# Layer 2 attention on one core: softmax halves merged on 32 partitions, three score buffers, all context keys made ahead

## The chip, the cores and the metric

The kernel runs on one core of a Trainium2 chip. The metric is the device time of one execution in microseconds (us); the time shown for a kernel is the median of its runs. A core has TensorE (PE in the profile, its weight loads PEld), VectorE (DVE), ScalarE (ACT), GpSimd (POOL) and SyncE (SP, which only issues DMAs here). Each works through its own instruction stream in order, and they wait for each other through semaphores. SBUF has 128 partitions; TensorE writes into PSUM[...].

## The reference

Four layers, each an attention and a feed-forward part with residuals, on x of 4x256x256 (batch, tokens, width) with a context of 4x1601x256. Only the attention of layer 2 is touched by the change:

```python
def _L2_xattn_ref(x, h_ctx_kv, wq, wk, wv, wo, wk_ctx, wv_ctx, q_norm_w, k_norm_w):
    # 16 query heads, 4 key heads, head width 128
    q = (x @ wq).reshape(B, L, NUM_HEADS, HEAD_DIM)
    k = (x @ wk).reshape(B, L, NUM_KV_HEADS, HEAD_DIM)
    v = (x @ wv).reshape(B, L, NUM_KV_HEADS, HEAD_DIM)
    q = rms_norm(q, q_norm_w)
    k = rms_norm(k, k_norm_w)
    k_ctx = (h_ctx_kv @ wk_ctx).reshape(B, T, NUM_KV_HEADS, HEAD_DIM)
    v_ctx = (h_ctx_kv @ wv_ctx).reshape(B, T, NUM_KV_HEADS, HEAD_DIM)
    k_ctx = rms_norm(k_ctx, k_norm_w)
    q = q * cos + rotate_half(q) * sin
    k = k * cos + rotate_half(k) * sin
    k_full = jnp.concatenate([k_ctx, k], axis=1)
    v_full = jnp.concatenate([v_ctx, v], axis=1)
    ...
    mask = jnp.concatenate([jnp.zeros((L, T), x.dtype), causal], axis=1)
    scores = jnp.einsum('blhd,bmhd->bhlm', q, k_full) * scale + mask
    probs = jax.nn.softmax(scores, axis=-1)
    out = jnp.einsum('bhlm,bmhd->blhd', probs, v_full)
    return out.reshape(B, L, NUM_HEADS * HEAD_DIM) @ wo
...
x = x + _L2_xattn_ref(_layernorm(x, axis=-1), ctx_2048, ...)
```

## The kernel before

Layer 2 attention is worked off in sixteen units, one for each batch entry and key head (`units`), with four query heads in each unit. The keys of a unit are 1601 of the context and 256 of its own, cut into 15 tiles of 128 (`NK2`); tiles 0 to 11 and 96 rows of tile 12 are context.

*Context keys made ahead.* `l2_early` is a generator that makes the context keys and values of the first 15 units (`EARLY`) in small pieces: products, norm, transposes, and stores to DRAM. Earlier layers call `fill` to run pieces of it beside their own work. What is left over runs while the first unit is prepared, and `for _ in self.early: pass` ends it before the first score.

*Preparation of a unit.* `prep` is a generator too: query products and their rope (two pieces, `tpq`), products of the own keys (`tpkv`, tiles 12 and 13, then 14), the square root for the norms, and transposes of the queries (`tpqT`) and the keys (`tpk`). A unit that was made ahead loads its context part from DRAM; the sixteenth makes it in `prep` itself, with six more `tpkv` and three more `tpk` pieces. While a unit's heads run, the pieces for the next unit are drawn by tables: `WHEN_EARLY` says how many in each of the eight steps (two steps for each head).

*A head.* Its 256 queries are worked in four chunks of 64 (`scores`, c from 0 to 3). The keys of a chunk are spread over partitions: four column groups of 32 in the array write four partition groups of a score tile (two PSUM banks), so each query's scores lie on four partitions, j, 32+j, 64+j and 96+j. VectorE adds the causal mask to the last tiles (L1489) and takes the maximum of each partition (L1492). ScalarE takes the exponential with that maximum and sums it (L1496). Maxima go to `nm`, sums to `sm`, both 128x8, a column for each group of 32 queries.

*The merge.* The four partial maxima and sums of a query have to be joined (`merge`). TensorE transposes `nm` and `sm` into PSUM (L1507, L1508). VectorE takes the smallest of the negated maxima (L1512) and differences (L1514); ScalarE exponentiates them (L1515); VectorE weights the sums, adds them, takes the reciprocal and multiplies (L1517 to L1521). TensorE transposes the result back (L1523) and VectorE copies it to `rm` (L1525). Then GpSimd scales the probabilities by `rm` (L1532, eight instructions a head), VectorE transposes them in blocks of 32x32 into `pT` (L1538), TensorE multiplies by the values (tile `o`), and after four heads `project` multiplies by `wo` and L1559 adds to the residual.

*Order.* The loop at the end of `l2_xattn` runs these beside each other: in each step the scores of one head, a step of the softmax of the head before it (`softmax_steps`), value products of the head before that (`value_steps`), and pieces of `prep`. The tile framework's scheduler then orders the instructions of each engine by its own estimate, except those that are pinned (`keep_in_program_order`). PSUM: two score tiles (four banks), two banks for `prep` and `project` (tag `tp`), one for the merge, one for `o`.

Of the kernel before, what the change touches and what calls it, by code (L numbers as in the profile page):

```python
# [23 lines left out]
P = 128  # L24
# [28 lines left out]
EARLY = 15  # L53
# [5 lines left out]
class Kernel:  # L59
# [1210 lines left out]
    def l2_xattn(self):  # L1270
# [11 lines left out]
        with ExitStack() as es:  # L1282
            one = es.enter_context(tc.tile_pool(name="a2one", bufs=1, reuse_waits="tile"))
            two = es.enter_context(tc.tile_pool(name="a2", bufs=2, reuse_waits="tile"))
            ps_s = es.enter_context(tc.tile_pool(name="a2s", bufs=2, space=PSUM))
            ps = es.enter_context(tc.tile_pool(name="a2p", bufs=2, space=PSUM))
            ps_m = es.enter_context(tc.tile_pool(name="a2m", bufs=1, space=PSUM))
# [6 lines left out]
            kw = one.tile([P, 1], F32, name="kw")  # L1294
            nc.scalar.dma_start(kw, i["l2_knw"].rearrange("o p -> p o"))
# [17 lines left out]
            def turned(b):  # L1313

                xn = self.xn.tile([P, 2, D], F32, name="xn")
                self.layernorm(xn, self.x[b])
                if b == 0:
                    self.fill(LN2)
                tp = ps.tile([P, 2, 2, P], F32, name="tp_ln", tag="tp")
                for k in range(2):  # L1320
                    for q in range(2):
                        nc.tensor.transpose(tp[:, k, q, :], xn[:, q, k * P : (k + 1) * P], self.ident)
                t = self.xnT.tile([P, 2, S], F32, name="xT2", tag="xnT")
                nc.scalar.copy(t, tp.rearrange("p k q t -> p k (q t)"))
                return t

            def swapped(ap):
# [5 lines left out]
            def load(g, early):  # L1333
                w = {}
                for n, shape in (("wq", [P, 2, 512]), ("wkc", [P, 2, 256]), ("wks", [P, 2, 256])):
                    if n == "wkc" and early:
                        continue
# [9 lines left out]
            def prep(u, w, ctxT, res):  # L1347
# [3 lines left out]
                early = u < EARLY  # L1351
                va = two.tile([P, NK, HD2], F32, name="va2", bufs=3)
                kT = two.tile([P, NK, P], F32, name="kT2")
                if early:
                    kd, vd = self.early_kv[u]
                    for t, d in ((kT, kd), (va, vd)):
                        nc.sync.dma_start(t[:, :CT, :], d[:, :CT, :])
                    nc.sync.dma_start(kT[:, CT, :96], kd[:, CT, :96])
                    nc.sync.dma_start(va[:96, CT, :], vd[:96, CT, :])
# [4 lines left out]
                kr = one.tile([P, NK, HD2], F32, name="kr2")  # L1364
                ss = self.small.tile([P, NK + 8], F32, name="ss2")
                ra, rb = tabs["l2_qnw"]
                qo = []
                for q in range(2):
# [6 lines left out]
                    nc.vector.tensor_reduce(ss[:, NK + 4 * q : NK + 4 * q + 4], sq, AX.X, ALU.add)  # L1375
# [11 lines left out]
                def squares(m0, m1):  # L1387
                    n = m1 - m0
                    sq = one.tile([P, 4, HD2], F32, name="sq2")
                    nc.scalar.activation(sq[:, :n, :], kr[:, m0:m1, :], AF.Square)  # L1390
                    nc.vector.tensor_reduce(ss[:, m0:m1], sq[:, :n, :], AX.X, ALU.add)

                if early:
                    nc.gpsimd.memset(kr[:96, CT, :], 0.0)
                for ms in ((12, 13), (14,), (0, 1), (2, 3), (4, 5), (6, 7), (8, 9), (10, 11)):
                    if early and ms[0] < CT:
                        continue
                    tp = ps.tile([P, 2, 256], F32, name="tpkv", tag="tp")
                    rows = P
                    for n, m in enumerate(ms):  # L1400
                        for k in range(2):
                            if m < CT:
                                self.mm(tp[:, n, :], ctxT[:, k, m * P : (m + 1) * P], w["wkc"][:, k, :], k == 0, k == 1)
                            elif m == CT and early:
                                pass
                            elif m == CT:
                                self.mm(tp[:96, n, :], ctxT[:, k, m * P : m * P + 96], w["wkc"][:, k, :], k == 0, k == 1)
# [3 lines left out]
                        if m == CT:  # L1411
                            for k in range(2):
                                self.mm(tp[96:, n, :], xb[:, k, :32], w["wks"][:, k, :], k == 0, k == 1)
                    m, n = ms[0], len(ms)
                    if m == CT and early:
                        for t, v in ((kr, tp[:, :, :HD2]), (va, tp[:, :, HD2:])):
                            nc.scalar.copy(t[96:, CT, :], v[96:, 0, :])
                            nc.scalar.copy(t[:, CT + 1, :], v[:, 1, :])
                    else:
                        nc.scalar.copy(kr[:rows, m : m + n, :], tp[:rows, :n, :HD2])  # L1420
                        nc.scalar.copy(va[:rows, m : m + n, :], tp[:rows, :n, HD2:])
                    if rows < P:
                        nc.gpsimd.memset(kr[rows:, m, :], 0.0)
                    if m == CT + 2:
                        ra, rb = tabs["l2_knw"]
                        ko = one.tile([P, 3, HD2], F32, name="ko2")
                        t2 = one.tile([P, 3, HD2], F32, name="kt2")
                        own = kr[:, CT:, :]
                        nc.gpsimd.tensor_tensor(ko, own, ra, ALU.mult)
                        nc.vector.tensor_tensor(halves(t2), swapped(own), halves(rb), ALU.mult)  # L1430
                        nc.gpsimd.tensor_tensor(ko, ko, t2, ALU.add)
                    if m in (2, 6, 10, 14):
                        squares(CT if m == 14 else m - 2, m + n)
                    yield
                m0 = CT if early else 0
                self.rstd(ss[:, m0:], ss[:, m0:], 1.0 / HD2, self.eps6)
                rq = two.tile([P, 8], F32, name="rq2")
                nc.vector.tensor_scalar(rq, ss[:, NK:], 1.0 / math.sqrt(HD2), None, ALU.mult)
# [4 lines left out]
                for m in range(0, 0 if early else CT, 4):  # L1443
                    nc.gpsimd.tensor_tensor(
                        kr[:, m : m + 4, :], kr[:, m : m + 4, :], ss[:, m : m + 4, None].to_broadcast([P, 4, HD2]), ALU.mult
                    )
                for m in range(3):
                    nc.scalar.activation(ko[:, m, :], ko[:, m, :], AF.Copy, scale=ss[:, CT + m : CT + m + 1])
# [8 lines left out]
                for m0 in (12,) if early else (0, 4, 8, 12):  # L1457
                    tp = ps.tile([P, 4, P], F32, name="tpk", tag="tp")
                    n = min(4, NK - m0)
                    for m in range(n):  # L1460
                        nc.tensor.transpose(tp[:, m, :], kr[:, m0 + m, :] if m0 < CT else ko[:, m, :], self.ident)
                    if m0 < CT:
                        nc.scalar.activation(kT[:, m0 : m0 + 4, :], tp, AF.Copy, scale=kw)
                    elif early:
                        nc.scalar.copy(kT[:, CT, 96:], tp[:, 0, 96:])
                        nc.scalar.copy(kT[:, CT + 1 :, :], tp[:, 1:n, :])
                    else:
# [772 lines left out]
```

## Time and profile before

| what | us |
|---|---|
| median of 3 runs | 2660.19 (2654.16 to 2660.89) |
| the profiled execution, time | 2609.97 |
| the profiled execution, span from first to last instruction | 2608.2 |
| layer 2 attention in it: first score 670.3, last residual add starts 1778.67 | about 1109 |
| the last context-key work of `l2_early` in it | to about 671 |

Times inside the kernel come from one profiled execution; its mean granted TensorE clock is 0.979. A residual add (L1559) closes each unit, so that the sixteen of them, at 780.0, 847.9, 917.3, 985.2, 1053.7, 1121.6, 1190.9, 1258.9, 1327.3, 1395.3, 1464.6, 1532.5, 1601.0, 1677.1, 1740.7 and 1778.7 us, mark the pace of the stage. Matmuls are pipelined in the records, so that a TensorE that shows as busy is not always streaming. A float32 matmul shows as two records.

### The profile page before, as it was taken

To read this page: it belongs to the slowest core of one execution; us is meant where nothing else is said; L and a number is where in the kernel's file an instruction comes from. 1 tells how busy PE (TensorE), PEld (TensorE's weight loads), DVE (VectorE), ACT (ScalarE), POOL (GpSimd) and SP (SyncE) were. 2 spreads that over 40 slices of the span, in tenths; PEclk is the share of its full clock that TensorE was granted. 3 is DMA by queue.
4 is the path that set the end of the run, shared out by engine and by line. 5 is a ranking of instruction groups with operands and counts; after the bars stand their busy time and mean duration, and the time that the engine had idled before them with its cause. 6 is when DMAs were issued, how large, how long until landed. Compare 5 with 4: busy or idle time off the path is not lost. (4 is left out here: it accounts for less than half of the span.)

```text
span 2608.2 us, 47024 instructions
## 1 busy us (share of the span) xinstructions
PE 2472.6 (95%) x17800; PEld 1512.2 (58%) x17816; DVE 1473.9 (57%) x3039; ACT 1307.1 (50%) x2955; POOL 751.9 (29%) x1030
## 2 busy tenths in 40 slices
PE   7989978999899999999999999998998999999997
PEld 4678967777455555555555555655564544545553
DVE  6344537635677777777777777673334314334323
ACT  2335545424544445444544454532326766857775
POOL 1015646132444334334334444332102001011000
PEclk8999999899999999999999999998999999999998
DMA  5155686626311111111111110004211100000000
GB/s 203 61 190 164 187 174 206 202 67 211 114 47 39 47 47 47 47 42 36 46 46 39 47 47 21 9 1 165 99 60 55 34 1 28 4 4 2 6 6 5
DMA packets 94654, 186.24 MB, mean 71 GB/s; under 512 B 15052, under 2 KB 62864, under 8 KB 93232
## 3 DMA queue, kind: packets, MB, share of 16 engines
q1 hardware_dynamic: 78278, 144.90, 16.4%
q0 software_dynamic: 10416, 28.46, 4.9%
q10 hardware_dynamic: 5738, 9.87, 1.2%
q8 instruction: 145, 2.38, 0.4%
q14 instruction: 77, 0.63, 0.1%
HBM read 136.77 MB, written 46.42 MB: 70 GB/s over the span
## 5 line engine op out<-in xcount | busy, mean ns | idle before, releaser
L1496 ACT ACTIVATE p<-s,nm 128x448 f32<-128x448 f32 (+1 forms) x512 | 326.9, 645 | 423.4 <-DVE nm L1492 259.1
L1957 ACT ACTIVATE e<-s 128x1024 f32<-128x1024 f32 (+1 forms) x448 | 404.3, 960 | 158.2 <-PE s L76 153.1
L76 PE MATMUL s<-kT,qT 128*32 128x448 f32 (+1 forms) x4096 | 470.2, 556 | 10.0 <-ACT p L1496 5.0
L76 PE MATMUL o<-pT,va 128*128 128x256 f32 (+2 forms) x1920 | 431.0, 376 | 6.1 <-DVE pT L1538 6.1
L1532 POOL TENSOR_SCALAR p<-p,rm 128x448 f32<-128x448 f32 (+1 forms) x512 | 323.3, 659 | 369.5 <-DVE rm L1525 339.2
L76 PEld LDWEIGHTS o<-pT,va 128*128 128x128 f32 (+1 forms) x1920 | 344.4, 191 | 93.0 <-issue 51.5
L1538 DVE STREAM_TRANSPOSE pT<-p 128x896 f32<-128x896 f32 (+1 forms) x256 | 283.8, 1127 | 37.2 <-POOL p L1532 33.5
L1492 DVE TENSOR_REDUCE nm<-s 128x2 f32<-128x896 f32 (+1 forms) x256 | 282.6, 1104 | 3.3
L76 PE MATMUL s<-qb,kT 32*128 32x256 f32 (+1 forms) x3328 | 267.6, 404 | 13.2 <-ACT e L1957 11.0
L76 PEld LDWEIGHTS s<-kT,qT 128*32 128x32 f32 x4096 | 123.6, 109 | 265.0 <-issue 223.4
L76 PE MATMUL o<-e,va 128*32 128x256 f32 (+1 forms) x3328 | 235.7, 391 | 1.2 <-DVE os L2054 1.2
L76 PEld LDWEIGHTS s<-qb,kT 32*128 32x128 f32 (+1 forms) x3328 | 162.9, 181 | 105.0 <-issue 75.4
L76 PEld LDWEIGHTS o<-e,va 128*32 128x32 f32 (+1 forms) x3328 | 90.5, 110 | 115.0 <-issue 74.9
L1984 POOL TENSOR_TENSOR x<-x,t 128x32 f32<-128x32 f32 x64 | 14.7, 252 | 438.4 <-DVE t L1979 438.4
L76 PE MATMUL fill<-wkc_early,ctxT 128*128 128x256 f32 (+1 forms) x532 | 130.7, 394 | 8.2 <-ACT kT_early L1252 7.8
L1489 DVE TENSOR_TENSOR s<-s,mask 128x128 f32<-128x128 f32 (+1 forms) x256 | 83.0, 325 | 67.5 <-PE s L76 62.8
L76 PEld LDWEIGHTS fill<-wkc_early,ctxT 128*128 128x128 f32 (+1 forms) x532 | 102.0, 196 | 26.2 <-ACT kT_early L1252 10.3
L431 POOL DMA_INDIRECT f0xr<-f0xd,f0src x95 | 92.0, 968 | 50.8 <-PE f0tph L488 42.3
L1384 POOL TENSOR_TENSOR qo<-qo,qt 128x512 f32<-128x512 f32 x32 | 41.1, 1284 | 225.2 <-DVE rm L1525 139.7
L1496 ACT ACTIVATION_READ_ACCUMULATOR p<-s,nm 128x1 f32 x512 | 101.7, 199 | 0.0
L76 PE MATMUL f2gu<-f2wgu,f2xsT 128*128 x176 | 85.6, 611 | 0.6 <-issue 0.3
L529 POOL DMA_INDIRECT f0yt<-f0yd,f0slot x64 | 66.8, 1044 | 47.5 <-DMA vd<-va_early 16.3
(517 smaller groups left out, 3567.4 us busy)
## 6 DMA issues: line engine op xcount, KB each, us to landing
ctxT<-in_ctxT SPq DMA_DIRECT2D x10, 1664.0 KB, 10.6
f0yd<-f0ys SPq DMA_DIRECT2D x95, 128.0 KB, 2.8
vd<-va_early SPq DMA_DIRECT2D x90, 128.0 KB, 2.5
kd<-kT_early SPq DMA_DIRECT2D x45, 256.0 KB, 2.5
kT<-kd SPq DMA_DIRECT2D x15, 768.0 KB, 4.2
va<-vd SPq DMA_DIRECT2D x15, 768.0 KB, 6.0
wq<-in_l_wq SPq DMA_DIRECT2D x16, 512.0 KB, 3.3
wo<-in_l_wo SPq DMA_DIRECT2D x16, 512.0 KB, 3.1
```

Source lines behind the costliest of these rows:

```text
L76: self.nc.tensor.matmul(out, lhsT, rhs, start=start, stop=stop, **kw)
L431: nc.gpsimd.indirect_dma_start(out=t, out_offset=None, in_=xd[:, :], in_offset=bass.IndirectOffsetOnAxis(ap=src[:, n : n + 1], axis=0),)
L529: nc.gpsimd.indirect_dma_start(out=yt, out_offset=None, in_=yd[:, :], in_offset=bass.IndirectOffsetOnAxis(ap=slot[:, t, r : r + 1], axis=0),)
L1384: nc.gpsimd.tensor_tensor(o1, o1, t2, ALU.add)
L1489: nc.vector.tensor_tensor(sv, sv, mask[:, 2 * c : 2 * c + 2, : nt - CT, :].rearrange("p n t i -> p n (t i)"), ALU.add)
L1492: nc.vector.tensor_reduce(nm[:, 2 * c : 2 * c + 2], s[:, :, : nt * 32], AX.X, ALU.max, negate=True)
L1496: nc.scalar.activation(p[:, n, : nt * 32], s[:, n, : nt * 32], AF.Exp, bias=nm[:, e : e + 1], accum_out=sm[:, e : e + 1],)
L1532: nc.gpsimd.tensor_scalar(p[:, n, : nt * 32], p[:, n, : nt * 32], r[:, e : e + 1], 1.0, ALU.mult, ALU.mult)
L1538: nc.vector.transpose(pT[:, 2 * c : 2 * c + 2, :nt, :].rearrange("p n t i -> p n (t i)"), p[:, :, : nt * 32])
L1957: nc.scalar.activation(e[:kr, :, :n, :], s[t][:kr, :, :n, :], AF.Exp, scale=1.0 / math.sqrt(HD3))
L1984: nc.gpsimd.tensor_tensor(xt, xt, t[:, q], ALU.add)
```

## The change

The merge no longer goes over TensorE. Maxima and sums of a head lie in one tile (`nmsm2`, 128x2x8). Four GpSimd copies bring its four partition groups side by side onto 32 partitions, VectorE and ScalarE join them there, and four GpSimd products write the shares `rm2` back to the four partition groups. The bank that the merge held, and one of the two of tag `tp`, make a third score tile. All sixteen units are made ahead, so that `prep` has no path of its own for context keys. The tables draw mostly one piece of `prep` per step. After each square root a tiny pinned exponential makes ScalarE load the exponential table at once.

```diff
-EARLY = 15
+EARLY = B * NKV2
...
-            ps_s = es.enter_context(tc.tile_pool(name="a2s", bufs=2, space=PSUM))
-            ps = es.enter_context(tc.tile_pool(name="a2p", bufs=2, space=PSUM))
-            ps_m = es.enter_context(tc.tile_pool(name="a2m", bufs=1, space=PSUM))
+            ps_s = es.enter_context(tc.tile_pool(name="a2s", bufs=3, space=PSUM))
+            ps = es.enter_context(tc.tile_pool(name="a2p", bufs=1, space=PSUM))
...
                 self.layernorm(xn, self.x[b])
+                exps_next()
...
+            def exps_next():
+
+                self.pin(nc.scalar.activation(self.small.tile([P, 1], F32, name="one2"), self.eps6, AF.Exp))
...
-                for ms in ((12, 13), (14,), (0, 1), (2, 3), (4, 5), (6, 7), (8, 9), (10, 11)):
-                    if early and ms[0] < CT:
-                        continue
+                for ms in ((12, 13), (14,)):
...
-                m0 = CT if early else 0
-                self.rstd(ss[:, m0:], ss[:, m0:], 1.0 / HD2, self.eps6)
+                self.rstd(ss, ss, 1.0 / HD2, self.eps6)
+                exps_next()
...
-            def merge(nm, sm):
-
-
-                t = ps_m.tile([P, 512], F32, name="tm2")
-                ct, st = t[:8, 0:P], t[:8, P : 2 * P]
-                tc.keep_in_program_order(nc.tensor.transpose(ct, nm, self.ident))
-                tc.keep_in_program_order(nc.tensor.transpose(st, sm, self.ident))
-                by = lambda ap: ap.rearrange("n (a j) -> n j a", a=4)
-                wide = lambda ap: ap[:, :, None].to_broadcast([8, 32, 4])
-                lo = self.small.tile([8, 32], F32, name="lo2")
-                nc.vector.tensor_reduce(lo, by(ct), AX.X, ALU.min)
-                e = self.small.tile([8, P], F32, name="em2", bufs=2)
-                nc.vector.tensor_tensor(by(e), wide(lo), by(ct), ALU.subtract)
+            def merge(ms):
+
+
+
+                c = self.small.tile([32, 4, 2, 8], F32, name="ms2")
+                for a in range(4):
+                    nc.gpsimd.tensor_copy(c[:, a], ms[32 * a : 32 * a + 32])
+                by = lambda ap: ap.rearrange("j a n -> j n a")
+                wide = lambda ap: ap[:, None, :].to_broadcast([32, 4, 8])
+                lo = self.small.tile([32, 8], F32, name="lo2")
+                nc.vector.tensor_reduce(lo, by(c[:, :, 0]), AX.X, ALU.min)
+                e = self.small.tile([32, 4, 8], F32, name="em2")
+                nc.vector.tensor_tensor(e, wide(lo), c[:, :, 0], ALU.subtract)
                 nc.scalar.activation(e, e, AF.Exp)
-                w = self.small.tile([8, P], F32, name="wm2", bufs=2)
-                nc.vector.tensor_tensor(w, e, st, ALU.mult)
-                tot = self.small.tile([8, 32], F32, name="tot2")
+                yield
+                w = self.small.tile([32, 4, 8], F32, name="wm2")
+                nc.vector.tensor_tensor(w, e, c[:, :, 1], ALU.mult)
+                tot = self.small.tile([32, 8], F32, name="tot2")
                 nc.vector.tensor_reduce(tot, by(w), AX.X, ALU.add)
                 nc.vector.reciprocal(tot, tot)
-                nc.vector.tensor_tensor(by(e), by(e), wide(tot), ALU.mult)
-                yield
-                nc.tensor.transpose(t[:, 256:264], e, self.ident[:8, :8])
                 r = self.small.tile([P, 8], F32, name="rm2")
-                nc.vector.tensor_copy(r, t[:, 256:264])
+                for a in range(4):
+                    nc.gpsimd.tensor_tensor(r[32 * a : 32 * a + 32], e[:, a], tot, ALU.mult)
                 return r
...
-            WHEN = [2, 2, 2, 3, 2, 0, 2, 2]
-            WHEN_EARLY = [0, 1, 1, 2, 1, 0, 2, 1]
-            BETWEEN = [0, 0, 0, 0, 0, 0, 1, 1]
+            WHEN = [0, 1, 1, 1, 2, 0, 1, 1]
+            BETWEEN = [0, 0, 0, 0, 0, 0, 0, 1]
...
-                        if pieces is not None and not early:
+                        if pieces is not None:
                             for _ in range(BETWEEN[step]):
                                 next(pieces, None)
```

## The prediction

> **What bounds the kernel now.** I read the page first, then a table of stretches, the waits, and the order of time inside one head. The page (busy time and share of each engine) and the table of stretches (length, then busy us of TensorE, weight loads, VectorE, ScalarE, GpSimd; clock, DMA share, GB/s), cut at the residual adds of L1559, which mark one unit each:
>
> ```profile
> PE 2472.6 (95%) x17800; PEld 1512.2 (58%) x17816; DVE 1473.9 (57%) x3039; ACT 1307.1 (50%) x2955; POOL 751.9 (29%) x1030
> ...
> 780.00:1601.00 821.00, 814.99 (x5240) 451.71 (x5236) 628.83 (x1063) 391.81 (x1104) 329.73 (x479) 1.00 0.13 44
> 1601.00:1677.10 76.10, 76.00 (x483) 46.84 (x479) 54.39 (x92) 36.24 (x102) 29.25 (x41) 1.00 0.02 7
> 1677.10:1740.70 63.60, 61.89 (x431) 35.57 (x427) 46.95 (x79) 28.01 (x81) 21.14 (x33) 1.00 0.03 9
> ```
>
> The first stretch is twelve units: 68.4 us each, TensorE covered 99% of the time, VectorE 52.4 us a unit. TensorE sets the pace, and the 76.1 us unit is the one in which the context keys of the last unit are made.
>
> The waits of VectorE in the middle of the stage, and one head in order of time (start, us, engine, line, operation, count, idle before and releaser):
>
> ```profile
> DVE wm L1517 <- ACT em L1515: 80.9, 50, 2.5
> ...
> 1126.57 0.29 ACT L1515 ACTIVATE em<-em 8x128 f32<-8x128 f32 x1
> 1126.89 0.28 DVE L1517 TENSOR_TENSOR wm<-em,tm 8x128 f32<-8x128 f32 x1 [1.40 <-ACT em L1515]
> 1127.20 0.38 DVE L1519 TENSOR_REDUCE tot<-wm 8x32 f32<-8x128 f32 x1
> 1127.90 0.99 PE L76 MATMUL s<-kT,qT 128*32 128x480 f32 x2
> 1128.82 0.22 PE L1523 MATMUL tm<-ident,em 8*128 8x8 f32 x1
> 1128.98 3.42 PE L76 MATMUL s<-kT,qT 128*32 128x480 f32 x30
> 1129.42 5.05 POOL L1532 TENSOR_SCALAR p<-p,rm 128x448 f32<-128x448 f32 x8 [8.96 <-DVE rm L1525]
> 1130.85 0.37 DVE L1489 TENSOR_TENSOR s<-s,mask 128x192 f32<-128x192 f32 x1 [1.59 <-PE s L76]
> 1131.12 1.10 DVE L1538 STREAM_TRANSPOSE pT<-p 128x896 f32<-128x896 f32 x1
> 1132.15 1.12 DVE L1492 TENSOR_REDUCE nm<-s 128x2 f32<-128x960 f32 x1
> 1134.47 1.12 DVE L1492 TENSOR_REDUCE nm<-s 128x2 f32<-128x960 f32 x1
> 1135.51 2.21 DVE L1538 STREAM_TRANSPOSE pT<-p 128x960 f32<-128x960 f32 x2
> 1137.12 0.21 ACT L1496 ACTIVATION_READ_ACCUMULATOR p<-s,nm 128x1 f32 x1
> ```
>
> Two things are to be seen. The merge's last transpose (tm) falls inside a run of score matmuls; the two chunks take from 1127.90 to 1132.33, 4.4 us, where an unbroken pair takes 3.43 (at 1109.99). And VectorE stands 1.4 us for the small exponential, which hurts nobody now.
>
> **What the Trainium skill says.** "TensorEngine Tiling (Array Packing)", Key Properties: changing the tiling mode drains TensorE; the trace agrees, a step between the 32-column scores and full-width work costs about 0.1 us beyond streaming. "GPSIMD Engine Reference", 3.1: two-input elementwise work costs about 2.6 cycles per element there, plus a dispatch per instruction. "ScalarE: Activation LUTs", What ACT_TABLE_LOAD costs: about 1283 ns a load, as here (1.28); its further 1.38 us drain is not visible here (load 1104.43, square root 1105.73).
>
> **The change, part by part.** I call T a transpose, k a mask add, M a maximum.
>
> *Off TensorE.* Per head two transposes (1123.52 to 1123.74, 0.22 us) and the third. In the built order of before, three heads of four have the third inside a quad of scores (cost 4.43-3.43 = 1.0 us), one has it between values (0.3). Per unit: 4x0.22+3x1.0+0.3 = 4.2 us. TensorE alone would then need about 64 us a unit.
>
> *VectorE's new order.* In the built program the five merge operations of a head (lo, em, wm, tot, reciprocal) stand in one piece, directly behind the head's last maximum and ahead of the T of that head and of the next masks. Before, they were spread over the next head's masks and maxima. So VectorE, in order, now waits out the whole chain: last exponentials, four GpSimd copies, em's exponential, then four GpSimd products and the first two scalings before the first T. That is a loop in which nothing of one head overlaps the next on VectorE. Its wait L, from the end of the last M to the first T:
> - exponentials of the last chunk: 0.11 to start plus 1.41 (1135.92 to 1137.33) = 1.52; semaphore 0.10
> - four copies of 32x16 on GpSimd. No row has them. GpSimd's 128x32 product takes 252 ns, two of them 0.46 us; 24 elements fewer at the skill's 2.6 cycles and 1.2 GHz is 0.05 less, so 0.16 start to start, 0.20 for the last: 0.7 (bounds 0.45 and 1.05)
> - VectorE's small work: the router's softmax (128x32 at 1794.67 to 1795.84) has the same operations: 0.22, 0.23, exponential 0.26, 0.23, 0.22, 0.20, plus 0.08 in: 1.44
> - 0.16 to GpSimd, four 32x8 products 0.67 (bounds 0.45 and 1.05), two scalings 1.26, hops 0.06: 2.15
>
> L = 1.52+0.10+0.70+1.44+2.15 = 5.9 us.
>
> Start to start a T is 1.03 (1131.12 to 1132.15) or 1.1 in the pair, a free k 0.27, k with its M behind it 0.37, M 1.04. A head's four T, four k, four M: 2.06+2.21+0.54+0.74+3.12+1.12 = 9.8 us. The four heads of a unit in the new order:
> - head 0: 9.8
> - head 1: plus two rounds of query work behind the first T, 6x0.6 (sum, two products): 13.4
> - head 2: one k and one M move in front of the first T, under L (-1.3); rope and squares of the own keys +1.1, reciprocal +0.2: 9.8
> - head 3: 9.8, its residual add hidden under L
>
> Sum 42.8. ScalarE delays two of the waits: in head 2 both table loads, the filler exponential (0.2) and three scalings of ko come ahead of the exponentials of chunks 2 and 3, +1.5; in head 3 a query copy stands ahead of the last, +0.5. Behind the copies and products on GpSimd nothing else is queued but this head's scalings; the two query scalings (1.04 each) that stand ahead of the copies in head 2 end within the +1.5. Layernorm once in four units: 0.7. Unit: 42.8+2.0+0.7+4x5.9 = 69.1, taken as 69.0, against 68.4. VectorE is late next, with TensorE some 4 us a unit idle. Where TensorE idles most: tpk's copy to kT now stands behind the merge's exponential, with only two value matmuls to cover it.
>
> *Third score buffer, single bank for prep pieces.* Nothing: no large wait on a score buffer before, and each prep piece has half a head to be emptied. TensorE's pieces find the bank free in the hand-made order by 0.3 us or more, except one (second query transpose, 1.4 us), inside TensorE's slack. Bounds -10 and +10 us.
>
> *Exponential table reloaded at once.* The same loads, earlier: the copies of ko stand between it and the maxima anyway. Counted in the +1.5.
>
> *Sixteenth unit early.* 52 matmul records (28 took 6.31 us, so 0.22 each) and 13 transposes at 0.11: 12.9 us ahead of the first score. The stretch 645 to 670 holds about 7 us in which TensorE waits for the prep of unit 0; I let 5 be filled: +8 (bounds +4 and +14; the last unit's norm and turns can stand alone). In return the 76.1 us unit becomes an ordinary one. SP's queue loses one context load and one weight load and gains this unit's stores and reads; the DMA share there is 2 to 13%, so I cost that at nothing.
>
> *Sum*, on the profiled execution (span 2608.2, time 2609.97). Before: first score 670.3 to the last residual add's end 1779.4, 1109.1. After: first head to its last M 8 (scores 1.7, four k and M 5.6, hops), fifteen units 15x69.0 = 1035.0, three heads without prep (14.4, 14.4, 15.7: one k and M hidden in the first two) 44.5, tail L 5.9 + T paced by the scalings 4.9 + values, projection, add as at 1767.55 to 1779.4, 11.8 = 22.6. Together 1110.1, +1; with the start +8: **+9**. The median shown, 2660.19, is 50 us above the profiled execution, for a reason that the profile doesn't give; I add the +9 to it: **2669**.
>
> **Rivals.** (1) *Faster: L is shorter than added up and TensorE's relief is passed on.* For it: small GpSimd memsets follow at 34 ns, and 4.2 us a unit are really gone from TensorE, the bound; were VectorE no bound, 15x4.2 would be saved. Against it: five engine hops remain. 63 heads turn on L, so 0.1 us is 6 us; it decides below L = 5.6. At L = 5.5: 9-25 = -16, 2644. If the timed runs are longer because TensorE's clock is lower in them, before is hurt more than VectorE's loop, which helps this case. (2) *GpSimd's small operations are dear*: 0.26 start to start, like its two memsets in a row (1106.31, 1106.57). Eight times 0.09 makes L 6.6: +41, in all +50, 2710. For it: partition moves, never seen here; against: the 128x32 product. (3) *The start doesn't hide*: +14 instead of +8, 2675; it shifts any case and is in the range.
>
> **How the numbers follow.** Forecast (L 5.6 to 6.3, difference -8 to +34; own range 2652 to 2694) 0.45, of it 0.17 within 8 us and 0.28 slower; rival 1 0.28; rival 2 0.27. What a measurement of this kernel can tell from no change is 0.3%, 8 us. So faster 0.28, same 0.17, slower 0.55. The range reaches from a little below rival 1 to rival 2: 2636 to 2712.
>
> **What would show it.** Right: VectorE waits of 2 us and more, once a head, for GpSimd's copies (before lo) and scalings (before the first T); units of 69 us with TensorE's coverage down by some 4 us each; no unit of 76 us; first score at about 678. Wrong: TensorE still without gaps and units of 67 us or less (rival 1); GpSimd copies 0.25 us apart (rival 2); VectorE's waits for TensorE's scores at the top.

## The result and the profile after

The changed kernel takes 2666.78 us in the median of 22 runs (2654.13 to 2671.25), the kernel before beside it 2658.49 us (22 runs). The ratio is **1.0032, 95% interval 1.0022 to 1.0041**: 8.3 us slower (5.8 to 10.9). That is about the 0.3%, 8 us, that the prediction took as the least that can be told from no change. A later group of runs (e11 below) gave 1.0033 (1.0022 to 1.0044), so the loss is small but real.

The profiled execution of the changed kernel has a span of 2666.0 us, that of the kernel before one of 2608.2. These 58 us aren't the effect of the change. The two programs are the same up to layer 2, and most of the difference is there: the first query product of layer 2 starts at 652.0 us before and at 695.7 us after. Two further profiles, of later groups (e8, the kernel before, 657.8; e11, the changed kernel, 658.7), show no such difference. The level ahead of layer 2 goes with the group of runs: each of the groups e1 to e4, e5 to e8 and e9 to e12 ran on one chip of its own, and this start is at 686 to 691 us in the first group and at 651 to 659 in the other two. Whether it is the chip or the hour that does it was not tried. So spans of different groups aren't compared below, only ratios to the kernel before on the same chip, and stretches of the trace that begin in layer 2.

The first line of the page of the changed kernel (busy time, share of the span and instructions of each engine):

```profile
PE 2448.7 (92%) x17609; PEld 1503.6 (56%) x17625; DVE 1397.0 (52%) x2912; ACT 1304.6 (49%) x2986; POOL 844.7 (32%) x1545
```

The table of stretches of the changed kernel, cut at the residual adds as for the kernel before (length, then busy us of TensorE, weight loads, VectorE, ScalarE, GpSimd; clock, DMA share, GB/s). The first line holds twelve units, the second and third one unit each:

```profile
839.70:1668.00 828.30, 773.40 (x5092) 435.43 (x5088) 574.01 (x966) 389.10 (x1119) 399.23 (x864) 1.00 0.14 44
1668.00:1734.70 66.70, 62.44 (x407) 35.64 (x407) 46.63 (x75) 31.32 (x91) 32.34 (x67) 1.00 0.04 14
1734.70:1803.40 68.70, 64.96 (x459) 36.70 (x451) 45.57 (x76) 25.36 (x78) 31.30 (x78) 1.00 0.03 8
```

A unit takes 828.30/12 = 69.03 us, where it took 68.42 before. TensorE is covered 93% of the stretch instead of 99%: it lost (814.99-773.40)/12 = 3.5 us of covered time per unit, and the unit still became longer. VectorE has less to do as well, 47.8 us per unit instead of 52.4. No engine is full any more, so something waits. The unit of 76.1 us is gone: the two stretches after the twelve take 66.7 and 68.7 us. VectorE's waits in the same twelve units of the changed kernel (total, times, longest):

```profile
DVE lo L1478 <- POOL ms L1474: 136.2, 48, 3.5
DVE pT L1503 <- POOL p L1497: 94.2, 48, 2.5
DVE wm L1484 <- ACT em L1481: 14.2, 48, 0.3
```

Each happens once a head, 48 times: 2.8 us until GpSimd's copies are done (which themselves wait for the head's last exponentials), 2.0 us for the scaled pieces, 0.3 us for the small exponential. Together they are 20.4 us per unit. With its 47.8 us of work VectorE is taken up for 68.2 of the 69.03 us: these waits are the pace. Before, the largest of its waits was 1.6 us per head for em's exponential (80.9 us in 50), which hurt nobody because TensorE was late.

One merge of the changed kernel in order of time (start, us, engine, line, operation, count, idle before and what ended it):

```profile
1194.72 1.16 DVE L1458 TENSOR_REDUCE nmsm<-s 128x2 f32<-128x960 f32 x1
...
1196.91 0.67 ACT L1462 ACTIVATE p<-s,nmsm 128x480 f32<-128x480 f32 x1
...
1197.74 0.88 POOL L1474 COPY ms<-nmsm 32x16 f32<-32x16 f32 x4 [7.67 <-ACT p L1462]
...
1198.65 0.20 DVE L1478 TENSOR_REDUCE lo<-ms 32x8 f32<-32x32 f32 x1 [2.77 <-POOL ms L1474]
...
1199.10 0.23 ACT L1481 ACTIVATE em<-em 32x32 f32<-32x32 f32 x1 [1.10 <-DVE em L1480]
...
1199.36 0.18 DVE L1484 TENSOR_TENSOR wm<-em,ms 32x32 f32<-32x32 f32 x1 [0.29 <-ACT em L1481]
...
1199.80 0.19 DVE L1487 RECIPROCAL tot<-tot 32x8 f32<-32x8 f32 x1
...
1200.14 0.96 POOL L1490 TENSOR_TENSOR rm<-em,tot 32x8 f32<-32x8 f32 x4 [1.52 <-DVE tot L1487]
...
1201.19 5.06 POOL L1497 TENSOR_SCALAR p<-p,rm 128x448 f32<-128x448 f32 x8
...
1202.49 1.11 DVE L1503 STREAM_TRANSPOSE pT<-p 128x896 f32<-128x896 f32 x1 [2.50 <-POOL p L1497]
...
1203.52 0.27 DVE L1455 TENSOR_TENSOR s<-s,mask 128x128 f32<-128x128 f32 x1
```

The last maximum ends at 1195.88 and the first transpose starts at 1202.49. In these 6.61 us VectorE works for 0.9 us. The next head's first scores, which TensorE began at 1199.71 (3.2 us for two chunks), lie ready from about 1201.3 (an estimate: half of the 3.2 us), but their mask stands behind that transpose in VectorE's order and runs at 1203.52.

### The profile page after: what moved, and what is told of

Same layout as the page of the kernel before. It is cut to its first block, busy times and chain, and to the rows that moved or that the text cites. A ratio compares the mean times of both kernels' runs of the same rounds, so it can differ in the third digit from the quotient of the medians.

```text
span 2666.0 us, 46991 instructions
## 1 busy us (share of the span) xinstructions
PE 2448.7 (92%) x17609; PEld 1503.6 (56%) x17625; DVE 1397.0 (52%) x2912; ACT 1304.6 (49%) x2986; POOL 844.7 (32%) x1545
## 5 line engine op out<-in xcount | busy, mean ns | idle before, releaser
L1462 ACT ACTIVATE p<-s,nmsm 128x448 f32<-128x448 f32 (+1 forms) x512 | 326.2, 644 | 511.6 <-DVE nmsm L1458 464.6
L76 PE MATMUL s<-kT,qT 128*32 128x448 f32 (+1 forms) x4096 | 433.1, 558 | 40.8 <-ACT p L1462 31.8
L76 PE MATMUL o<-pT,va 128*128 128x256 f32 (+2 forms) x1920 | 438.9, 380 | 6.4 <-DVE pT L1503 4.9
L1458 DVE TENSOR_REDUCE nmsm<-s 128x2 f32<-128x896 f32 (+1 forms) x256 | 283.1, 1110 | 4.5
L76 PE MATMUL fill<-wkc_early,ctxT 128*128 128x256 f32 (+1 forms) x584 | 150.1, 406 | 9.2 <-ACT kT_early L1252 8.6
L1474 POOL COPY ms<-nmsm 32x16 f32<-32x16 f32 x256 | 48.3, 189 | 314.5 <-ACT p L1462 306.6
L76 PEld LDWEIGHTS fill<-wkc_early,ctxT 128*128 128x128 f32 (+1 forms) x584 | 115.6, 202 | 31.4 <-ACT kT_early L1252 12.4
L1462 ACT ACTIVATION_READ_ACCUMULATOR p<-s,nmsm 128x1 f32 x512 | 101.5, 198 | 0.0
L1478 DVE TENSOR_REDUCE lo<-ms 32x8 f32<-32x32 f32 x64 | 12.4, 193 | 170.0 <-POOL ms L1474 170.0
L1490 POOL TENSOR_TENSOR rm<-em,tot 32x8 f32<-32x8 f32 x256 | 50.2, 196 | 117.1 <-DVE tot L1487 105.8
L1455 DVE TENSOR_TENSOR s<-s,mask 128x128 f32<-128x128 f32 (+1 forms) x256 | 79.0, 313 | 11.0 <-PE s L76 10.9
```

The source lines that it names most:

```text
L76: self.nc.tensor.matmul(out, lhsT, rhs, start=start, stop=stop, **kw)
L1455: nc.vector.tensor_tensor(sv, sv, mask[:, 2 * c : 2 * c + 2, : nt - CT, :].rearrange("p n t i -> p n (t i)"), ALU.add)
L1458: nc.vector.tensor_reduce(ms[:, 0, 2 * c : 2 * c + 2], s[:, :, : nt * 32], AX.X, ALU.max, negate=True)
L1462: nc.scalar.activation(p[:, n, : nt * 32], s[:, n, : nt * 32], AF.Exp, bias=ms[:, 0, e : e + 1], accum_out=ms[:, 1, e : e + 1],)
L1474: nc.gpsimd.tensor_copy(c[:, a], ms[32 * a : 32 * a + 32])
L1478: nc.vector.tensor_reduce(lo, by(c[:, :, 0]), AX.X, ALU.min)
```

## The experiments

Every ratio is to the kernel before, run beside it. "Unit" is the mean of the twelve intervals between residual adds from the first to the thirteenth; "start" is the time from the first query product of layer 2 to the first score; "first add" is the first residual add of layer 2.

| kernel | ratio (95%) | start | first score to first add | unit | first to last add |
|---|---|---|---|---|---|
| before (e8) | | 18.4 | 109.7 | 68.42 | 998.8 |
| changed | 1.0032 (1.0022, 1.0041) | 34.2 | 109.8 | 69.03 | 995.2 |
| changed again (e11) | 1.0033 (1.0022, 1.0044) | 32.5 | 109.1 | 68.94 | 995.5 |
| e1 merge late | 0.9970 (0.9958, 0.9981) | 32.5 | 107.8 | 67.31 | 973.1 |
| e2 before, 16 early | 1.0045 (1.0031, 1.0059) | 34.1 | 114.5 | 68.44 | 988.0 |
| e3 changed, old merge | 1.0061 (1.0044, 1.0077) | 34.8 | 113.3 | 68.92 | 995.5 |
| e4 changed, pools of before | 1.0092 (1.0075, 1.0108) | 36.1 | 116.3 | 69.01 | 995.5 |
| e5 merge spread | 0.9791 (0.9770, 0.9811) | 34.2 | 100.6 | 65.22 | 940.6 |
| e6 copies doubled | 1.0099 (1.0076, 1.0123) | 32.5 | 108.1 | 69.90 | 1011.0 |
| e7 no reload | 1.0065 (1.0046, 1.0084) | 30.8 | 108.4 | 69.82 | 1005.3 |
| e9 spread, pieces early | **0.9708** (0.9687, 0.9729) | 34.2 | 98.7 | 63.72 | 920.9 |
| e10 old merge, no reload | 1.0055 (1.0036, 1.0075) | 33.5 | 111.7 | 68.93 | 995.6 |
| e12 e9, pools of before | 0.9756 (0.9732, 0.9781) | 36.1 | 106.4 | 64.09 | 926.8 |

**Does VectorE's place for the merge set the unit? (e1)** The reduction lo and the product wm are tied behind what the source has ahead of them on VectorE, and the merge's steps are taken later in the next head.

```diff
-                nc.vector.tensor_reduce(lo, by(c[:, :, 0]), AX.X, ALU.min)
+                self.pin(nc.vector.tensor_reduce(lo, by(c[:, :, 0]), AX.X, ALU.min))
...
-                nc.vector.tensor_tensor(w, e, c[:, :, 1], ALU.mult)
+                self.pin(nc.vector.tensor_tensor(w, e, c[:, :, 1], ALU.mult))
...
                             hd["p"].append(scores(kT, qT, h, cc, hd["ms"]))
-                        if soft is not None:
-                            next(soft[0])
+                            if soft is not None and cc > 0:
+                                next(soft[0])
```

(The step that was taken at the end of the first half falls away, and the first of the four transposes is tied behind the fourth maximum.)

> The changed kernel with its merge moved on VectorE: lo and em stand behind the next head's first two maxima, wm to reciprocal behind its third, the transposes behind its fourth; nothing is added or left out. Loop theory (VectorE waits out the merge's chain once a head, 5 to 6 us, and this sets the unit at 69.0 us): the waits of 3.5 us for GpSimd's copies and 2.5 us for the scalings fall below 1 us, TensorE is the bound again without the split quads, units of 64 to 66 us, some -50 us against the changed kernel, ratio to the kernel before 0.980 to 0.990. Rival, TensorE is held by something else (one bank for all prep pieces, score buffers): units stay at 68 to 69 us, ratio 1.000 to 1.004.

The unit fell to 67.31 us and the ratio to 0.997: the order matters, but less than the loop theory said, and neither theory's number came. Some waits of e1 in twelve units say why:

```profile
DVE pT L1503 <- POOL p L1497: 112.3, 96, 3.4
...
DVE s L1455 <- PE s L76: 57.8, 36, 2.9
PE o L76 <- DVE pT L1503: 33.1, 48, 1.6
PEld o L76 <- DVE pT L1503: 21.7, 12, 2.1
```

The wait for GpSimd's copies ahead of lo is gone from the list, so the loop was broken there. Now TensorE waits for the transposes ahead of the values, since the four of them stand in one block of 5.0 us at the end of VectorE's head.

**The same with the merge spread evenly (e5).** One step of the merge behind each of the next head's four maxima: lo and em, then wm to the reciprocal, then two transposes, then two. The edit against the changed kernel, without the two ties of lo and wm, which are those of e1, and without the steps behind the last head:

```diff
-                nc.vector.transpose(
+                self.pin(nc.vector.transpose(
...
                     turn(hd["p"][c], hd["pT"], c)
-                yield
+                    if c % 2:
+                        yield
...
                             hd["p"].append(scores(kT, qT, h, cc, hd["ms"]))
-                        if soft is not None:
-                            next(soft[0])
+                            if soft is not None:
+                                next(soft[0])
...
-                        if soft is not None and c == 0:
-                            next(soft[0])
```

> The changed kernel with its merge spread over the next head's four chunks on VectorE: lo and em behind the first maximum, wm to reciprocal behind the second, two transposes behind the third and two behind the fourth; nothing is added or left out. In e1 the values waited for the four transposes, which stood in one block behind the fourth maximum (1.5 us ahead of the values behind the own keys, 12 times, and 0.4 us 72 times). If that block is what kept the unit at 67.3 us, units of 64.5 to 66 us and a ratio of 0.985 to 0.992. Rival, another wait of the same size takes over: 67 us or more, ratio 0.995 to 0.999.

The unit is 65.22 us, as expected; the ratio, 0.9791, is lower than that, since the first add (100.6 us after the first score, 109.8 in the changed kernel) and the last units with the stretch behind them gain too. No operation was added to the changed kernel or taken from it: the same instructions in another order take 3.8 us less per unit. Moving the merge moves its parts on other engines too: ScalarE's small exponential, a query product of GpSimd's and a few value matmuls stand elsewhere in a unit of e5. VectorE's waits for GpSimd's copies and scaled pieces are gone from its list altogether. What is left in twelve units of e5:

```profile
DVE s L1455 <- PE s L76: 113.7, 69, 3.4
...
PEld s L76 <- ACT kT L1434: 22.6, 12, 1.9
PE s L76 <- ACT kT L1434: 19.7, 12, 1.6
```

VectorE waits for TensorE's scores, so TensorE is the bound again. Once a unit TensorE stands some 1.6 us for ScalarE's copy of the next unit's keys.

**That last wait taken away (e9).** The last prep pieces move half a head forward:

```diff
-            WHEN = [0, 1, 1, 1, 2, 0, 1, 1]
-            BETWEEN = [0, 0, 0, 0, 0, 0, 0, 1]
+            WHEN = [0, 1, 1, 1, 2, 0, 1, 0]
+            BETWEEN = [0, 0, 0, 0, 0, 0, 1, 1]
```

> e5 with the next unit's last three prep pieces half a head earlier: both query transposes in the seventh step, the key transposes ahead of the last values. In e5 TensorE stood 1.8 us per unit between tpk and the next unit's first scores, for the copy of the keys. If nothing else takes that place, units of 63.3 to 63.8 us instead of 65.2 and a ratio 0.010 lower than e5, 0.966 to 0.972. Rival, the single prep bank makes the second query transpose wait for the first one's copy and gives the gain back: units of 64.5 us or more, ratio 0.976 or more.

Unit 63.72 us, ratio 0.9708: the first alternative, and the fastest kernel of this study. The stretch of twelve units:

```profile
789.40:1554.00 764.60, 764.60 (x5088) 438.52 (x5088) 575.28 (x965) 390.06 (x1120) 401.84 (x864) 1.00 0.15 48
```

TensorE is covered without a gap. This is what the change, with the pieces moved, takes off TensorE: 68.42-63.72 = 4.7 us per unit. Most of it was there from the beginning; the order kept it from being seen.

**Is each 0.1 us of the merge's chain worth 6 us? (e6)**

```diff
+                c0 = self.small.tile([32, 4, 2, 8], F32, name="ms20")
+                for a in range(4):
+                    nc.gpsimd.tensor_copy(c0[:, a], ms[32 * a : 32 * a + 32])
                 c = self.small.tile([32, 4, 2, 8], F32, name="ms2")
                 for a in range(4):
-                    nc.gpsimd.tensor_copy(c[:, a], ms[32 * a : 32 * a + 32])
+                    nc.gpsimd.tensor_copy(c[:, a], c0[:, a])
```

> The changed kernel with a second set of four GpSimd copies of 32x16 between the maxima and lo (the partial results go through one more tile); the value computed is the same. Loop theory: the wait L from the last maximum to the first transpose grows by 0.9 us in each of 63 heads, units of 69.0 + 4 x 0.9 = 72.6 us, ratio 1.003 + 0.021 = 1.024. Rival, VectorE's wait is only partly on the path: units below 71 us, ratio below 1.015.

The unit grew by 0.87 us, not by 3.6: the rival's side. The waits of VectorE in twelve units of e6, to be read against those of the changed kernel above:

```profile
DVE lo L1481 <- POOL ms L1477: 169.0, 48, 4.2
DVE pT L1506 <- POOL p L1500: 72.3, 48, 2.5
```

The first wait grew by 32.8 us, 0.68 us per head or 2.7 us per unit: four more copies cost 0.68 us there, not 0.9. The two sets of copies in one head of e6:

```profile
1194.58 0.92 POOL L1474 COPY ms<-nmsm 32x16 f32<-32x16 f32 x4 [3.09 <-ACT p L1462]
1195.56 0.60 POOL L1477 COPY ms<-ms 32x16 f32<-32x16 f32 x4
```

The first set reads four partition groups and its copies start 0.24 us apart, the second stays on the same 32 partitions and its copies start 0.14 us apart. VectorE's second wait shrank by 21.9 us, 1.8 us per unit. In this build the first query work of the next unit (sum and two products, 1.9 us) stands ahead of the first transpose in one head of each unit, where in the changed kernel it stands behind it in all units but one of these, so it is done inside the wait. 2.7-1.8 = 0.9 us is what was measured. So the loop holds by the waits, and the count of 6 us for each 0.1 us does not: the length of the chain can't be changed alone, since the order around it answers, and that was left out of the expectation.

**What do the sixteen early units cost? (e2, e8, e11)** e2 is the kernel before with one edit; e8 and e11 are the two kernels themselves.

```diff
-EARLY = 15
+EARLY = B * NKV2
```

> The kernel before with nothing but the sixteenth unit's context keys made early. The last unit gives back 7.6 us (76.1 to about 68.5) under both theories. Start hides in part, as predicted (+8): ratio 1.000. Start does not hide (+12 to +16): ratio 1.002 to 1.003, with the first score 12 to 16 us later than in a profile of before in the same condition.

> The kernel before itself, for a second profile of it. If the profile shown was one of an unusual execution ahead of layer 2, the first query product of layer 2 starts at 685 to 696 us here, as in the other profiles, instead of 652; from it to the first score 18 us and from the first to the last residual add 999 us as in the profile shown. Rival: the early start belongs to the kernel before and the changed kernel lost 40 us ahead of layer 2, then it starts at 652 again.

> The changed kernel itself, for a second profile of it on the chip of this call. From the first query product of layer 2 to the first score 34 us, units of 69.03 us, from the first to the last residual add 995 us, as in its first profile; ratio 1.002 to 1.005. Against it: the 34 us belong to the one execution, and 26 us are seen as predicted (18 + 8).

The start takes 34.1 us in e2, 34.2 and 32.5 us in the changed kernel, 18.3 and 18.4 us before: 14 to 16 us more in place of 8. In e2 this is set against 10.8 us from the first to the last add, which the unit without its late context keys gives back, and the ratio is 1.0045: on its own this part of the change loses. It loses more than the 1.002 to 1.003 expected for a start that doesn't hide, for the first add of e2 comes another 4.8 us later after the first score (114.5 against 109.7), and the stretch behind the last add is 5.5 us longer (835.1 against 829.6); why is open. e8's first query product stood at 657.8 us, outside the range that was expected, and so did those of e5 to e7: the early start belongs to neither of the two kernels, and neither alternative had that. The stretch from the first query product to the first score in e8, the kernel before:

```profile
657.80:676.20 18.40, 14.90 (x63) 9.26 (x61) 6.69 (x12) 10.97 (x29) 10.60 (x12) 0.91 0.72 236
```

and in e11, the changed kernel:

```profile
658.60:691.10 32.50, 28.68 (x133) 19.23 (x131) 10.33 (x20) 22.11 (x55) 15.48 (x18) 1.00 0.74 247
```

TensorE is free for 3.5 us in the first and for 3.8 us in the second. Early key work covers 3.9 us of TensorE in e8 and 17.1 us in e11 (each matmul counted up to the start of the next). There was nothing to hide the 13 us under.

**The merge, the pools and the reload apart (e3, e4, e7, e10).** e3 is the changed kernel with the three TensorE transposes of before, two score buffers, two prep banks and a bank for the merge. e4 is the changed kernel with its own merge and with two score buffers and two prep banks. e7 and e10 are the changed kernel and e3 without the two small exponentials.

```diff
 e3
-            ps_s = es.enter_context(tc.tile_pool(name="a2s", bufs=3, space=PSUM))
-            ps = es.enter_context(tc.tile_pool(name="a2p", bufs=1, space=PSUM))
+            ps_s = es.enter_context(tc.tile_pool(name="a2s", bufs=2, space=PSUM))
+            ps = es.enter_context(tc.tile_pool(name="a2p", bufs=2, space=PSUM))
+            ps_m = es.enter_context(tc.tile_pool(name="a2m", bufs=1, space=PSUM))
...
+                nm, sm = ms[:, 0], ms[:, 1]
+                tc.keep_in_program_order(nc.tensor.transpose(ct, nm, self.ident))
...
 e4
-            ps_s = es.enter_context(tc.tile_pool(name="a2s", bufs=3, space=PSUM))
-            ps = es.enter_context(tc.tile_pool(name="a2p", bufs=1, space=PSUM))
+            ps_s = es.enter_context(tc.tile_pool(name="a2s", bufs=2, space=PSUM))
+            ps = es.enter_context(tc.tile_pool(name="a2p", bufs=2, space=PSUM))
...
 e7, e10
-                exps_next()
...
-                exps_next()
```

> The changed kernel with the merge of before put back (three transposes on TensorE, two score buffers, two prep banks and one bank for the merge), the sixteenth early unit and the table reload kept. Loop theory: units back to 68.4 us, 15 x 0.6 = 9 us less than the changed kernel, ratio about 1.000. Rival, the new merge costs nothing in total and the whole difference is the start: ratio stays 1.003.

> The changed kernel with two score buffers and two prep banks as before, the merge and the rest as changed. If the third score buffer and the single bank are worth nothing, as predicted, units of 69.0 us and ratio 1.003 plus or minus 0.001. Rival: the third buffer hides part of VectorE's stall from TensorE, without it units of 70 us or more, ratio 1.009 or more; or the single prep bank costs, and the ratio falls below 1.001.

> The changed kernel without the two small exponentials that bring the exponential table back behind each square root (their results are used by nothing). As predicted, the reload costs and brings nothing: units of 69.0 us, ratio 1.003. Rival: e3 stood at 68.9 us a unit against 68.4 in e2 although both have the merge of before, and the reload is the cause: units of 68.5 us, ratio 1.000.

> e3 (the changed kernel with the merge of before) without the two small exponentials that bring the table back. e3 stood at 68.92 us a unit against 68.44 in e2. If the reload costs with the merge of before, units of 68.4 to 68.5 us; if the new steps of the prep pieces cost it, units of 68.9 us or more.

- e3 against e4: the same 995.5 us from the first to the last add. In the order that the changed kernel has, the new merge is worth nothing in the ordinary units. It is two bounds of one length: in twelve units of e3 TensorE is covered for 823.11 of 827.01 us, in e4 VectorE has the waits of the changed kernel. e3's unit of 68.92 us, above e2's 68.44, is not the reload's doing (e10: 68.93). In e3 the merge's third transpose splits a run of scores in 48 heads of 48, in the kernel before in 36: the changed steps of the prep pieces moved the fourth head's transpose among the scores. At 1.1 us for a split (measured in the last section) that is 1.1 us per unit; measured are 0.5, so other moves give some of it back. Which ones was not tried.
- e4 against the changed kernel: the units are alike (69.01 and 69.03), but the first add comes 152.4 us after the first query product instead of 144.0. The third score buffer and the single prep bank, changed together here, are worth 8.4 us at the start of the stage (the changed kernel again, e11, has 141.6). The ratios differ by 0.006, some 16 us; 4.5 of the rest lie behind the last add (835.6 us to the end of the span against 831.1), and what the others are is open.
- e7: without the reload a unit takes 69.82 us, 0.8 us more, and the ratio is 1.0065. ScalarE in one unit of e7:

```profile
1202.11 0.30 ACT L80 ACTIVATE ss<-ss,eps 128x11 f32<-128x11 f32 x1
1203.64 1.28 ACT L1460 ACT_TABLE_LOAD   x1 [1.23 <-DVE nmsm L1456]
1204.94 0.66 ACT L1460 ACTIVATE p<-s,nmsm 128x480 f32<-128x480 f32 x1
```

The table is loaded only when the maximum has come, in the middle of the chain that VectorE waits out: the longest wait for the copies is 4.4 us instead of 3.5. VectorE's and GpSimd's order in a unit is the same in both kernels. With the merge of before, where TensorE sets the pace, the reload makes no difference (e10 and e3).

**Are the third buffer and the single bank needed once the order is mended? (e12)** It is e9 with the pools of before, the edit of e4.

> e9 with two score buffers and two prep banks as before. If the third buffer matters only where VectorE does not set the pace, units rise by 1 us or more over e9, to 64.5 us or more; if it matters only at the start of the stage (as e4 says, 8 us from the first query product to the first residual add), units stay within 0.3 us of e9 and the ratio rises by 0.003.

The unit rises by 0.37 us and the first add comes 142.5 us after the first query product instead of 132.9. The unit lies a little outside the 0.3 us of the second alternative and short of the 1 us of the first, and the ratio rises by 0.005 instead of 0.003: the pools matter at the start of the stage, here for 9.6 us, and less in all the units after it (926.8 us from the first to the last add against 920.9).

## Why the prediction was right, and where its terms were not

The forecast of 2669 us against 2666.78, and of +9 us against +8.3, is right, and so is its mechanism: the merge in one piece makes VectorE wait, and this sets a unit of 69 us. That the numbers meet so closely is luck. The start was 6 to 8 us worse than forecast, the stage behind it 4 to 5 us better, and the 69.0 us is itself a sum of errors that cancel. The pools, counted at nothing, hold the result where it is: with the pools of before (e4) the same change measures 1.0092, some 24 us instead of 8.

- *VectorE becomes the bound, by waiting.* Right. The unit is 69.03 us (forecast 69.0), the waits stand where they were said to stand, and they fall out of the trace when the order is changed (e5; in e1 the first of them). The place at which TensorE idles most is another than forecast: in twelve units its score matmuls wait 20.0 us for exponentials of earlier scores, and 5.1 us for the copy to kT.
- *TensorE is relieved by 4.2 us per unit and would need about 64.* Right: 63.72 us in e9, where the prep pieces are moved as well.
- *L = 5.9 us.* Too short: 6.33 us in the heads without a delay (2.49 to lo, 1.34 to the end of the reciprocal, 2.50 to the transpose). GpSimd is the term: its four copies take 0.88 us instead of 0.70 and its four products 0.96 instead of 0.67. The length of one operation was right: a last product was to take 0.20 us, an estimate from the 2.6 cycles per element of the Trainium skill, "GPSIMD Engine Reference", 3.1, and it takes 0.20. What failed is the step from one to the next: 0.05 us was taken off the 0.21 us at which two 128x32 products follow each other before, to 0.16, but the copies follow at 0.23 us and the products at 0.25. In e6 the copies that stay on their partitions follow at 0.14, so that moving data between partitions, which rival 2 named, is the likely cause; no run varies that alone. (For the copies the price was not the fitting one in any case: the page gives 2.6 cycles for two inputs, and a copy of 32x16 has one input and 16 elements per partition.) L lies at the upper edge of the forecast's band of 5.6 to 6.3, and nearer to rival 2's 6.6 than to 5.9. Four heads make this +1.7 us per unit.
- *ScalarE's delays of 2.0 us per unit.* 1.3 us: the wait before lo is 1.06 us longer in the head with the table loads and 0.28 us in the one with the query copy. The rest of the sum, 43.5 us with the layernorm, was therefore about 1.1 us too high. So the 69.0 is right by luck, as a total of three errors that cancel (+1.7, -0.7, -1.1).
- *The reload counts nothing.* It is worth 0.8 us per unit (e7). The argument that the copies of ko stand between the load and the maxima anyway failed: in e7 the first exponential comes ahead of these copies and waits for the load.
- *Third score buffer and single bank: nothing.* Right for the units (e4), wrong at the start of the stage, 8 us; by the ratios of e4 and the changed kernel it is some 16 us in all, more than the bounds of 10 us that were given.
- *Start +8, of it 5 us hidden.* This step failed. It is +14 to +16, the third rival's value. (The first score at about 678, which was to be a sign, isn't seen as such: it stands at 729.9 us, and at 691.2 in e11, because the level ahead of layer 2 moved as well.) The 7 us in which TensorE was said to wait for the prep of unit 0 were not there; the table of stretches of the kernel before has for that place:

```profile
645.00:670.00 25.00, 21.21 (x95) 14.71 (x93) 11.11 (x26) 15.45 (x41) 10.59 (x12) 0.93 0.73 240
```

  That is 3.8 us free, and the changed kernel leaves as much free after the keys are put in (3.8 us in e11), since it waits at other places for GpSimd and ScalarE. So nothing was hidden.
- *From the first score to the last residual add +1.* It is -3.4 us: 1105.8 us to the end of the add, where 1110.1 were summed. The first of the fifteen units takes 59.2 us and not 69.0 (the other fourteen mean 69.0): VectorE has 41.0 us of work in it where an ordinary one has 46.3, since query work of the next unit and a residual add don't fall in it, and it stands free for 18.2 us instead of 22.4, since the merges of the first heads lie among other work. Besides, the first head took 10.2 us instead of 8, the last three 48.7 instead of 44.5, the tail 21.6 instead of 22.6. The kernel before has the same short first unit (59.5), which a sum per unit doesn't see.
- *Which path made the two meet.* +14 to +16 from the start, -3.4 to -3.8 in the stage and +1.2 to +1.5 behind the last add (829.6 us to the end of the span before, 830.8 and 831.1 after) give +11.5 to +14 by the two traces of the changed kernel; the timed difference is 8.3 (5.8 to 10.9). Where the 1 to 8 us between them lie is open. The part ahead of layer 2 isn't in this sum, and by itself it differs by up to 7 us between the profiles of the last two groups (651.2 us in e5, 658.7 in e11).
- *Rivals.* The first needed L under 5.6; its price for TensorE's relief was sound, and it came true once the merge was moved (e5, e9). The second took 0.26 us from one small GpSimd operation to the next; the products come to 0.25 and the copies to 0.23, close to its sign of 0.25, and L to 6.33 of its 6.6. Its price was added up too low: 63 heads at 8 times 0.09 us are 45 us, not 41. By the same count L = 5.6 means -10 us, not the -8 at which the forecast's band began.

## What to carry to other kernels

Where an in-order engine has to hand small pieces through two other engines and back, count the chain once per turn of the loop and ask what stands behind it on that engine. Then look for a place where each hop lies under work that is there anyway. Here the same instructions cost 69.0 us per unit in one piece and 65.2 us when spread over the next head. Before work is moved to a "free" place at a stage's start, sum the gaps of the bound engine there: 13 us of keys went to a place with under 4 us of gaps and were paid in full.

## What the runs showed of the hardware that had not been expected

- GpSimd operations of 32 partitions by 8 or 16 elements show 0.19 to 0.20 us each, but it is the step from one start to the next that counts: 0.23 to 0.24 us for copies that take another partition group each, 0.25 us for the products that write to one each, and 0.14 us for e6's copies of the same shape that stay on the same 32 partitions. So four of the latter cost 0.60 us, of the former 0.88 to 0.92. That the move between partitions makes the difference is likely, but no run varies it alone.
- A run of scores that is split by one small transpose costs TensorE much more than the transpose. In the twelve units before, two chunks of scores of one shape take 3.36 us from their first matmul to the next other work where nothing splits them (12 times), and 4.43 us in 33 of the 36 heads in which the merge's third transpose does: 1.1 us more, of which the transpose itself has 0.15. One of the unsplit ones, to be read against the three lines from 1127.90 on in the prediction:

```profile
1109.99 3.43 PE L76 MATMUL s<-kT,qT 128*32 128x480 f32 x32
1113.35 1.13 PE L76 MATMUL o<-pT,va 128*128 128x256 f32 x4
```

- A table load of 1.28 us that comes early by a small exponential whose result nothing uses is worth 0.8 us per unit (e7) when the first real user stands in a chain that an in-order engine waits out, and nothing when it doesn't (e10 against e3). The Trainium skill, "ScalarE: Activation LUTs", What ACT_TABLE_LOAD costs, gives 1283 ns for the load, and the mean in the traces is 1283 ns before and after.
